# Graph-attention layers on one core: second-layer weights in one VectorE pass, their target factors in values and sum columns, folding on TensorE, and a new step order

## The chip, the cores and the metric

The kernel runs on one core of a Trainium2 chip. Its engines are TensorE (PE in the profile; PEld is its weight load), VectorE (DVE), ScalarE (ACT), GpSimd (POOL) and SyncE (SP), which here only issues transfers. The metric is the device time of one execution in microseconds, lower is better. A comparison counts as a difference from about 0.2% on.

## The reference, cut to what matters

64 graphs of 256 nodes and 512 features go through three attention layers with one shared adjacency `adj` per graph. All is float32.

```python
# layer 0: 8 heads of 64
Q, K, V = x @ W_q + b_q, x @ W_k + b_k, x @ W_v + b_v
scores  = Q K^T / 8 + (x @ w_g[:D])[:, None] + (x @ w_g[D:])[None, :] + log(adj + 1e-9)
x = softmax(scores) V + x
# graph attention, called twice: 8 heads (W1), then 1 head (W2)
h = layer_norm(x) @ W ;  s = h . a_src ;  t = h . a_dst        # per head
e = leaky_relu(s[:, None] + t[None, :], 0.2) + adj
x = softmax(e) h + x
```

Below these are "layer 0", "layer 1" (8 heads) and "layer 2" (one head); the "second layer" of the title is layer 1.

## The kernel before

**A softmax without maxima.** The exponential of leaky_relu(s + t) is max(exp(s + t), exp(0.2 (s + t))). A factor that depends only on the row i (the source, s) drops out of a softmax over j. Dividing by exp(s) leaves, for target j and row i, the larger of e1 = exp(t_j) and e2 R = exp(0.2 t_j) exp(-0.8 s_i), times EA = exp(adj). The rows R = exp(-0.8 s) are made by `target_rows` (L393 to 410): TensorE transposes the column s (called `ends`), ScalarE takes the exponential, the row goes to DRAM and comes back spread over all partitions. The weight tile is made in the transposed position (j on partitions): for each of 8 heads and each half of j ScalarE computes relu(e2 R - e1) (L601), and VectorE adds e1 and multiplies by EA (L605). Layer 2 does it in VectorE alone (L651, L654).

**Sums and values.** `weight_sums` (L338 to 366) lets TensorE multiply weight tiles by columns of ones (`onehot`), 32 columns at a time, so that the sums of eight heads land in one bank; VectorE takes the reciprocal (L355), which goes through DRAM and returns as R, spread over the partitions of each head (L362). `weigh` (L368) multiplies weights by values on TensorE (`num`), and VectorE multiplies by R (L385) and adds bias and residual (L387), giving yT or zT. `tokens` transposes back for the statistics of the layer norm (bn_stats L252, aggregate, variance; a power on POOL, L226), whose result `rstd` scales what leaves the next product.

**Products of 512 x 512 weights** run as seven half-size products instead of eight (`winograd`, L270 to 320). Four sums of blocks of the left factor come from POOL (`left_factors`, L255), those of the weights from `combine` (L94) once. Products 1, 5, 2, 6 and 3 form one step, 7 and 4 one step each. ScalarE copies a partial product out of PSUM ("kept", L467, L490, L560), so that product 6 waits for the copy of product 1; VectorE adds two partial products ("put", L476, L484, L532, L569). Product 4 leaves through ScalarE (L567). For layers 1 and 2 copies and puts also scale by `rstd`.

**Folding.** The layer norm's gain g, bias b and mean are folded into W1 and W2 once, by `fold_norm` (L127 to 216): scaled, the column mean subtracted, two extra columns per head (W times a_src and a_dst) appended, so that s and t come out of the same product as h. Nearly all of that is VectorE work, and it stands in graph 0, ahead of its first use.

**Order.** `graph(b)` is a generator that yields after each step, from "load" to "product 2". TensorE executes steps in an order written by hand, `period`: pairs of an age and a step, so that graphs of six ages, -1 to 4, are in flight in one period. The first and last graphs use the same list with the missing ages left out. Other engines' order is decided by a scheduler, which also assigns buffers[...]. Buffers that matter here: four ET buffers shared by layer 0 and layer 1, eight PSUM banks for everything, four "kept" buffers, and two o2 buffers, shared by the output tile and the final checks. The checks of the range of sums and exponents (L716 to 729) come last and decide how many graphs a plain second pass repeats; here none.

## Time and profile before

| | |
|---|---|
| time, median of 3 | 3669.86 us (3669.45 to 3669.88) |
| span of the profiled run | 3667.4 us |
| chain that ended last, by engine | PE 74%, DVE 17%, ACT 4%, POOL 2%, issue 2%, DMA 1% |
| DMA, mean over the span | 102 GB/s, 32% of 16 engines |
| largest group on ScalarE | L601, 1024 x 597 ns |
| largest group on VectorE | L605, 1024 x 550 ns |
| largest on TensorE | L378, `num`, 4096 records of 382 ns |

How to read it. The records of matmuls overlap[...]: their mean length is longer than the distance from start to start (a product of two 128 x 128 x 264 matmuls has four records, lasts 1.05 us and is followed 0.89 us later by the next one). So busy time is a union, and how long work takes is read from starts. The waits of an engine are listed apart, each with what ended it. A line of a helper (`winograd`, `tokens`) stands for several layers; tiles tell them apart: `wq`, `wk`, `wv` and `w` (layers 1 and 2, 264 and 257 columns wide).

### The profile page before, as it was taken

How to read it: one execution, taken by the hardware profiler on the slowest of the kernel's cores; microseconds unless marked ns; L12 is line 12 of the kernel's file. 1: busy time of each engine (PE TensorE's matmuls, PEld its weight loads, DVE VectorE, ACT ScalarE, POOL GpSimd, SP SyncE). 2: the span in 40 equal slices, each digit the busy share in tenths (PEclk: the TensorE clock that was granted, in tenths of full speed). 3: DMA queues.
4: the chain of work that ended last, by engine and by line, in shares of the span. 5: the costliest groups of instructions: out<-in, count | busy, mean ns of one | idle time of the engine just before them, and what ended most of it. 6: DMA issues, size and time to landing. Idle time of an engine off the chain costs nothing.

```text
span 3667.4 us, 75964 instructions
## 1 busy us (share of the span) xinstructions
PE 3496.0 (95%) x29969; PEld 2907.1 (79%) x29969; DVE 2531.1 (69%) x6015; ACT 1549.5 (42%) x3717; POOL 678.7 (19%) x981
## 2 busy tenths in 40 slices
PE   6989999999999999999999999999999999999995
PEld 5778888888888888888888888888888888888874
DVE  7676676677677667667667766766766766676675
ACT  2434444444444444444444444444444444444441
POOL 1111121121111111111111111211211111111120
PEclk9999999999999999999999999999999999999998
DMA  4323333333323323333333333333333233233331
GB/s 129 94 86 106 101 106 102 105 101 104 107 93 113 106 91 113 103 96 111 100 102 111 97 106 102 103 105 102 103 102 107 94 112 106 90 114 102 97 101 56
DMA packets 202332, 373.90 MB, mean 102 GB/s; under 512 B 21554, under 2 KB 119410, under 8 KB 201972
## 3 DMA queue, kind: packets, MB, share of 16 engines
q1 hardware_dynamic: 198084, 367.67, 31.9%
q8 instruction: 239, 3.92, 0.4%
q10 hardware_dynamic: 3888, 1.32, 0.2%
q14 instruction: 121, 0.99, 0.1%
HBM read 266.61 MB, written 102.31 MB: 101 GB/s over the span
## 4 chain that ended last, share of the span: by engine, by line
PE 74%; DVE 17%; ACT 4%; issue 2%; POOL 2%; DMA 1%; SPq 0%; ACTq 0%; DVEq 0%; POOLq 0%
PE ps_a L286 15%; PE ps_a L293 13%; PE ps_num L378 12%; PE ps_b L286 8%; PE ps_b L293 6%; PE ps_sc L507 5%; PE ps_su L349 3%; PE ps_av L664 3%; DVE ET L517 3%; PE ps_c L286 3%; PE ps_c L293 3%; DVE ET L605 2%; DVE st L252 2%; DVE X L622 2%; ACT ET L514 2%
## 5 line engine op out<-in xcount | busy, mean ns | idle before, releaser
L601 ACT ACTIVATE ET<-R,ne,e 128x256 f32<-128x256 f32 x1024 | 537.5, 597 | 85.9 <-PE ps_num L378 75.8
L605 DVE SCALAR_TENSOR_TENSOR ET<-ET,e,EA 128x256 f32<-128x256 f32 x1024 | 537.2, 550 | 0.2 <-ACT ET L601 0.2
L378 PE MATMUL ps_num<-ET,V 128*64 128x256 f32 x4096 | 470.3, 382 | 0.0
L378 PEld LDWEIGHTS ps_num<-ET,V 128*64 128x64 f32 x4096 | 282.4, 137 | 158.3 <-DVE var L224 18.9
L385 DVE TENSOR_TENSOR ps_num<-ps_num,R 128x512 f32<-128x512 f32 x256 | 177.3, 693 | 314.1 <-PE ps_num L378 187.3
L517 DVE TENSOR_TENSOR ET<-ET,AT 128x1024 f32<-128x1024 f32 x256 | 307.9, 1223 | 92.3 <-ACT ET L514 92.1
L286 PE MATMUL ps_a<-w,S 128*128 128x264 f32 (+1 forms) x1024 | 276.0, 392 | 42.2 <-ACT m L560 42.2
L265 POOL TENSOR_TENSOR S<-yT 128x256 f32<-128x256 f32 x128 | 95.7, 747 | 1059.8 <-DVE yT L387 1049.8
L514 ACT ACTIVATE ET<-ps_sc 128x512 f32<-128x512 f32 x512 | 270.4, 600 | 45.4 <-PE ps_sc L507 45.4
L286 PE MATMUL ps_b<-w,S 128*128 128x264 f32 (+1 forms) x1024 | 268.8, 385 | 16.7 <-DVE w L97 16.7
L286 PE MATMUL ps_a<-w,yT 128*128 128x264 f32 (+1 forms) x1024 | 280.6, 396 | 3.7 <-DVE V L569 3.7
L286 PEld LDWEIGHTS ps_a<-w,S 128*128 128x128 f32 x1024 | 179.6, 190 | 107.7 <-ACT m L560 67.5
L664 PE MATMUL ps_av<-V,ET 128*128 128x258 f32 (+1 forms) x1024 | 248.5, 387 | 11.2 <-DVE ET L654 11.2
L507 PE MATMUL ps_sc<-QT,KT 64*128 64x256 f32 x2048 | 255.7, 389 | 0.0
L560 ACT ACTIVATE m<-ps_a,rstd 128x257 f32<-128x257 f32 (+1 forms) x128 | 61.3, 479 | 457.8 <-POOL rstd L226 240.8
L349 PE MATMUL ps_su<-ET,onehot 128*32 128x128 f32 x8192 | 251.3, 275 | 0.0
L349 PEld LDWEIGHTS ps_su<-ET,onehot 128*32 128x32 f32 x8192 | 216.8, 110 | 29.9 <-issue 21.7
L286 PEld LDWEIGHTS ps_b<-w,S 128*128 128x128 f32 x1024 | 195.1, 191 | 48.4 <-issue 17.4
L664 PEld LDWEIGHTS ps_av<-V,ET 128*128 128x128 f32 x1024 | 198.5, 194 | 42.1 <-DVE ET L654 6.4
L286 PEld LDWEIGHTS ps_a<-w,yT 128*128 128x128 f32 x1024 | 179.3, 190 | 60.5 <-issue 36.2
L507 PEld LDWEIGHTS ps_sc<-QT,KT 64*128 64x128 f32 x2048 | 187.3, 186 | 46.8 <-issue 22.1
L262 POOL TENSOR_TENSOR S<-yT 128x256 f32<-128x256 f32 x128 | 93.7, 732 | 661.4 <-PE ps_a L286 496.2
(161 smaller groups left out, 6440.3 us busy)
## 6 DMA issues: line engine op xcount, KB each, us to landing
xT<-kept SPq DMA_DIRECT2D x128, 512.0 KB
R<-kept SPq DMA_DIRECT2D x256, 256.0 KB
R<-kept SPq DMA_DIRECT2D x128, 512.0 KB
X<-in_x_dram SPq DMA_DIRECT2D x64, 512.0 KB
kept<-xT SPq DMA_DIRECT2D x64, 512.0 KB
kept<-yT SPq DMA_DIRECT2D x64, 512.0 KB
out_dram<-o SPq DMA_DIRECT2D x128, 256.0 KB
A<-in_adj_dram SPq DMA_DIRECT2D x64, 256.0 KB
```

The lines of the kernel that those rows point to most:

```text
L265: nc.gpsimd.tensor_tensor(s3, a11, a21, ALU.subtract)
L286: nc.tensor.matmul(to, A[:, kk, :], B[:, kk, :], start=(first and kk == 0), stop=(kk == 1), skip_group_check=not first,)
L293: nc.tensor.matmul(to[:, m * P : (m + 1) * P], B[:, kk, m * P : (m + 1) * P], A[:, kk, :], start=(first and m == kk == 0), stop=(kk == 1), ...
L349: nc.tensor.matmul(pt[32 * g : 32 * g + 32, :P], onehot[:, i, :], pair[h // 4][:, j, h % 4, o : o + P], start=(i == j == 0), stop=(i == 3 ...
L378: nc.tensor.matmul(at[i * DH : (i + 1) * DH, :], V[:, j, h // 4, h % 4 * DH : (h % 4 + 1) * DH], pair[h // 4][:, j, h % 4, :], start=(j == ...
L385: nc.vector.tensor_tensor(both, both, R[:, m0 : m0 + 2, :], ALU.mult)
L507: nc.tensor.matmul(banks[h % 2][:, o : o + N], KT[lo : lo + DH, (q + h) // 2, j * P : (j + 1) * P], QT[lo : lo + DH, (q + h) // 2, :], sta ...
L514: nc.scalar.activation(ET[:, j, i::2, :], banks[i].rearrange("p (h n) -> p h n", n=N), AF.Exp)
L517: nc.vector.tensor_tensor(ET[:, j, :, :], ET[:, j, :, :], AT[:, j, :].unsqueeze(1).to_broadcast([P, 4, N]), ALU.mult,)
L601: nc.scalar.activation(e, R[q][:, h, :], AF.Relu, scale=e2[:, j, at : at + 1], bias=ne1[:, j, at : at + 1],)
L605: nc.vector.scalar_tensor_tensor(e, e, e1[:, j, at : at + 1], EA[:, j, :], ALU.add, ALU.mult)
L664: nc.tensor.matmul(av[:, :width], ET[:, j, t * P : (t + 1) * P], V2[:, j, n, :width], start=(j == 0), stop=(j == NT - 1),)
```

## The change

It has five parts.

1. **Weights of layer 1 in one pass.** Dividing also by exp(0.2 t_j) leaves max(R, f) EA with f = exp(0.8 t_j): one VectorE operation, no ScalarE one. The missing factor exp(0.2 t_j) belongs to the target, the contracted index: it is multiplied into the values V1 (four VectorE operations a graph) and into the columns that TensorE sums with (`factor_columns`, filled by ScalarE, two sets used in turn). In layer 2 it goes into EA (two ScalarE operations), and the weights are one operation for each half.
2. **Layer 0.** AT = adj + 1e-9 is now a ScalarE operation; exp(c), which was a factor of AT, becomes the bias of the scores' exponential. The range check reads the sums in PSUM rather than their reciprocals.
3. **Folding on TensorE.** `fold_norm` becomes a generator of three steps ("transpose", "columns", "totals"): W is transposed on TensorE to multiply it by a_src and a_dst, sums over rows for bias and mean are matmuls, and VectorE scales and subtracts in one operation per block. The vectors a_src and a_dst come as columns, and POOL spreads them.
4. **Step order.** A new `period`, a written list `start` for the first steps (with the folding in it) and a list `finish` for the last ones.
5. **The range checks** stand after "rows 2" of the last graph rather than after everything.

The diff, cut to its core:

```diff
-    onehot = const.tile([P, 4, 32], F32, name="onehot")
-    nc.gpsimd.memset(onehot, 0.0)
-    for i in range(4):
-        nc.gpsimd.memset(onehot[:, i, 8 * i : 8 * i + 8], 1.0)
+    def sum_columns(name, n):
+        t = const.tile([P, 24 + 32 * n], F32, name=name)
+        nc.gpsimd.memset(t, 0.0)
+        return t, t[:, 24:].rearrange("p (n c) -> p n c", c=32)[:, :, :8]
+    ones, eights = sum_columns("ones", 1)
+    nc.gpsimd.memset(eights, 1.0)
+    factor_columns = [sum_columns(f"factors{i}", NT * H) for i in range(2)]
+    filled = [None, None]
...
+            vectors = const.tile([P, KC, 2, heads], F32, name=f"vectors{name}")
+            nc.gpsimd.memset(vectors, 0.0)
+            for i, a in enumerate((sources, targets)):
+                a = load_columns(f"a{i}{name}", a.rearrange("h d -> (h d)"))
+                for h in range(heads):
+                    lo, hi = (h % 2 * DH, h % 2 * DH + DH) if heads > 1 else (0, P)
+                    chunk = slice(h // 2, h // 2 + 1) if heads > 1 else slice(0, KC)
+                    nc.gpsimd.tensor_copy(vectors[lo:hi, chunk, i, h], a[lo:hi, chunk])
+            yield
+            wT = work.tile([P, KC, D], F32, name="wT", tag="ET", bufs=4)
+            for m in range(KC):
+                pt = ps("fold")
+                for kc in range(KC):
+                    block = w[:, BLOCKS[kc // 2, m // 2], kc % 2, m % 2 * P : m % 2 * P + P]
+                    nc.tensor.transpose(pt[:, kc * P : (kc + 1) * P], block, ident)
+                nc.scalar.copy(wT[:, m, :], pt)
+            yield
+            pt = ps("fold")
+            more = w.shape[-1] - HD
+            products = pt[:, : KC * 2 * heads].rearrange("p (k n) -> p k n", k=KC)
+            for kc in range(KC):
+                for m in range(KC):
+                    nc.tensor.matmul(
+                        products[:, kc, :], wT[:, m, kc * P : (kc + 1) * P],
+                        vectors[:, m].rearrange("p i h -> p (i h)"),
+                        start=(kc == m == 0), stop=(m == KC - 1), skip_group_check=True,
+                    )
+            for (k, n), at in BLOCKS.items():
+                nc.vector.tensor_copy(
+                    w[:, at, :, HD:], products[:, 2 * k : 2 * k + 2, n * more : (n + 1) * more]
+                )
+            yield
+            columns, means = (
+                work.tile([P, KC, P], F32, name=n, tag="o2") for n in ("columns", "means")
+            )
+            nc.scalar.copy(columns, b.unsqueeze(2).to_broadcast([P, KC, P]))
+            nc.scalar.mul(means, g.unsqueeze(2).to_broadcast([P, KC, P]), 1.0 / D)
+            got = {}
+            for what, left in (("row", columns), ("mean", means)):
                 for n in range(2):
-                    part = acc[:, n * HD : (n + 1) * HD]
+                    pt = got[what, n] = ps(what)[:, : HD + more]
                     for kc in range(KC):
-                        block = w[:, BLOCKS[kc // 2, n], kc % 2, :HD]
-                        if kc == 0:
-                            nc.vector.tensor_scalar(part, block, scale(kc), None, ALU.mult)
-                        else:
-                            nc.vector.scalar_tensor_tensor(
-                                part, block, scale(kc), part, ALU.mult, ALU.add
-                            )
-                pt = ps("fold")
-                nc.tensor.matmul(pt, ones, acc, start=True, stop=True)
-                return pt
+                        nc.tensor.matmul(
+                            pt, left[:, kc, :], w[:, BLOCKS[kc // 2, n], kc % 2, :],
+                            start=(kc == 0), stop=(kc == KC - 1),
+                        )
...
+            for kc in range(KC):
+                for n in range(2):
+                    block = w[:, BLOCKS[kc // 2, n], kc % 2, :]
+                    nc.vector.scalar_tensor_tensor(
+                        block, block, g[:, kc : kc + 1], got["mean", n], ALU.mult, ALU.subtract
+                    )
+            combine(w)
...
-        def weight_sums(pair):
+        def weight_sums(pair, columns):
...
+                        t, at = columns(j, h)
                         nc.tensor.matmul(
-                            pt[32 * g : 32 * g + 32, :P], onehot[:, i, :],
+                            pt[32 * g : 32 * g + 32, :P], t[:, at - 8 * i : at - 8 * i + 32],
...
-            note(inverse, 0)
+            note(pt[:, :P], 0)
...
-            for j in range(NT):
-                nc.vector.tensor_scalar(
-                    AT[:, j, :], pt[:, j * N : (j + 1) * N], 1e-9, ec[:, j : j + 1],
-                    ALU.add, ALU.mult,
-                )
+            nc.scalar.activation(AT.rearrange("p j n -> p (j n)"), pt, AF.Identity, bias=eps)
...
-                            ET[:, j, i::2, :], banks[i].rearrange("p (h n) -> p h n", n=N), AF.Exp
+                            ET[:, j, i::2, :], banks[i].rearrange("p (h n) -> p h n", n=N), AF.Exp,
+                            bias=c[:, j : j + 1],
...
-            e1 = small.tile([P, NT, H], F32, name="e1", tag="e1")
-            nc.scalar.activation(e1, ends[:, :, 1, :], AF.Exp)
-            e2 = small.tile([P, NT, H], F32, name="e2", tag="e2")
-            nc.scalar.activation(e2, ends[:, :, 1, :], AF.Exp, scale=0.2)
-            ne1 = small.tile([P, NT, H], F32, name="ne1", tag="ne1")
-            nc.vector.tensor_scalar(ne1, e1, -1.0, None, ALU.mult)
+            f = small.tile([P, NT, H], F32, name="f", tag="f")
+            nc.scalar.activation(f, ends[:, :, 1, :], AF.Exp, scale=0.8)
+            factors, factors8 = factor_columns[b % 2]
+            filled[b % 2] = b
+            for j in range(NT):
+                nc.scalar.activation(
+                    factors8[:, j * H : (j + 1) * H, :],
+                    ends[:, j, 1, :].unsqueeze(2).to_broadcast([P, H, 8]), AF.Exp, scale=0.2,
+                )
+                for n in range(2):
+                    v = V1[:, j, n, :HD].rearrange("p (h d) -> p h d", d=DH)
+                    at = j * H + n * H // 2
+                    nc.vector.tensor_tensor(
+                        v, v, factors8[:, at : at + H // 2, :1].to_broadcast([P, H // 2, DH]), ALU.mult
+                    )
...
-                        e, at = ET[:, j, h, :], 4 * q + h
-                        nc.scalar.activation(
-                            e, R[q][:, h, :], AF.Relu, scale=e2[:, j, at : at + 1],
-                            bias=ne1[:, j, at : at + 1],
-                        )
+                        at = 4 * q + h
                         nc.vector.scalar_tensor_tensor(
-                            e, e, e1[:, j, at : at + 1], EA[:, j, :], ALU.add, ALU.mult
+                            ET[:, j, h, :], R[q][:, h, :], f[:, j, at : at + 1], EA[:, j, :],
+                            ALU.max, ALU.mult,
                         )
...
-            R = weight_sums(pair)
+            assert filled[b % 2] == b
+            R = weight_sums(pair, lambda j, h: (factors, 24 + 32 * (j * H + h)))
...
+            f = small.tile([P, NT], F32, name="f2", tag="f2")
+            nc.scalar.activation(f, ends[:, :, 1, 0], AF.Exp, scale=0.8)
+            factor = small.tile([P, NT], F32, name="factor", tag="factor")
+            nc.scalar.activation(factor, ends[:, :, 1, 0], AF.Exp, scale=0.2)
+            for j in range(NT):
+                nc.scalar.mul(EA[:, j, :], EA[:, j, :], factor[:, j : j + 1])
...
-                nc.vector.tensor_scalar(
-                    ET[:, j, :], R[0][:, 0, :], e2[:, j : j + 1], e1[:, j : j + 1], ALU.mult, ALU.max
+                nc.vector.scalar_tensor_tensor(
+                    ET[:, j, :], R[0][:, 0, :], f[:, j : j + 1], EA[:, j, :], ALU.max, ALU.mult
                 )
-            nc.vector.tensor_tensor(ET, ET, EA, ALU.mult)
...
-            (4, "V2 7"), (2, "rows 1"), (0, "Q"), (3, "weights"), (0, "Q7"), (4, "V2 4"),
-            (3, "weights"), (4, "rows 2"), (4, "weights 2"), (3, "weights"), (0, "Q4"),
-            (2, "weights"), (1, "product 0"), (-1, "load"), (0, "K"), (0, "K7"), (3, "sums 1"),
-            (1, "tokens 1"), (0, "K4"), (0, "scores"), (3, "product 1"), (1, "V1"), (1, "V1 7"),
-            (4, "product 2"), (0, "V"), (1, "V1 4"), (0, "scores"), (0, "V7"), (2, "weights"),
-            (4, "product 2"), (-1, "transpose x"), (3, "tokens 2"), (2, "weights"), (2, "weights"),
-            (0, "V4"), (0, "sums 0"), (3, "V2"), (2, "weights"),
+            (0, "transpose x"), (3, "weights"), (3, "weights"), (3, "weights"), (4, "V2 7"),
+            (0, "Q"), (3, "weights"), (4, "V2 4"), (3, "weights"), (0, "Q7"), (2, "weights"),
+            (4, "rows 2"), (1, "product 0"), (0, "Q4"), (0, "K"), (0, "K7"), (-1, "load"),
+            (3, "sums 1"), (3, "product 1"), (1, "tokens 1"), (4, "weights 2"), (0, "K4"),
+            (0, "scores"), (1, "V1"), (4, "product 2"), (3, "tokens 2"), (1, "V1 7"), (0, "V"),
+            (0, "scores"), (0, "V7"), (3, "V2"), (0, "V4"), (4, "product 2"), (2, "weights"),
+            (1, "V1 4"), (0, "sums 0"), (1, "rows 1"), (2, "weights"),
...
+        start = [
+            (0, "load"), (0, "transpose x"), (0, "Q"), (0, "Q7"), (0, "Q4"), (0, "K"), (0, "K7"),
+            (0, "K4"), (0, "scores"), (0, "V"), (1, "load"), (0, "scores"), ("w1", "transpose"),
+            ("w1", "columns"), (1, "transpose x"), ("w1", "totals"), (0, "V7"), (0, "V4"),
+            (0, "sums 0"), (1, "Q"), (1, "Q7"), (0, "product 0"), (1, "Q4"), (1, "K"), (1, "K7"),
+            (2, "load"), (0, "tokens 1"), (1, "K4"), (1, "scores"), ("w2", "transpose"), (0, "V1"),
+            ("w2", "columns"), (0, "V1 7"), (1, "V"), (1, "scores"), (1, "V7"), (1, "V4"),
...
+        finish = [
+            (-4, "rows 1"), (-5, "weights"), (-2, "transpose x"), (-5, "weights"), (-5, "weights"),
+            (-5, "weights"), (-6, "V2 7"), (-2, "Q"), (-5, "weights"), (-6, "V2 4"),
+            (-5, "weights"), (-2, "Q7"), (-4, "weights"), (-6, "rows 2"), (-3, "product 0"),
+            (-2, "Q4"), (-2, "K"), (-2, "K7"), (-1, "load"), (-5, "sums 1"), (-5, "product 1"),
...
+            (-2, "V2 4"), (-1, "weights"), (-2, "rows 2"), (-1, "sums 1"), (-1, "product 1"),
+            (-2, "weights 2"), (-2, "product 2"), (-1, "tokens 2"), (-1, "V2"), (-2, "product 2"),
+            (-1, "V2 7"), (-1, "V2 4"), (-1, "rows 2"), (-1, "weights 2"), (-1, "product 2"),
+            (-1, "product 2"),
+        ]
+        whole = start + order[len(start) - len(FOLDS) : len(order) - len(finish)]
+        whole += [(B + g, name) for g, name in finish]
...
+                if (g, name) == (B - 1, "rows 2"):
+                    worst = small.tile([P, 1], F32, name="worst", tag="worst")
+                    for v in (top, bottom):
+                        over = work.tile([P, P + 4 * H], F32, name="over", tag="o2")
+                        nc.gpsimd.memset(over, 0.0)
+                        note_odd(over[:, :P], v[:, :P], 1e-25, 1e25)
+                        note_odd(over[:, P:], v[:, P:], -60.0, 60.0)
+                        nc.vector.tensor_reduce(worst, over, AX.X, ALU.max)
+                        nc.vector.tensor_tensor(odd, odd, worst.to_broadcast([P, NT]), ALU.max)
...
```

## The prediction

> **What bounds the kernel now.** I read the engine totals first, then the same totals cut into three stretches, then who TensorE waits for in each stretch, and last the order of events in one period.
>
> ```profile
> PE 3496.0 (95%) x29969; PEld 2907.1 (79%) x29969; DVE 2531.1 (69%) x6015; ACT 1549.5 (42%) x3717; POOL 678.7 (19%) x981
> ```
>
> ```profile
> 0.00:227.84 227.84, 180.50 (x1420) 150.73 (x1420) 159.62 (x377) 77.57 (x187) 35.55 (x60) 0.94 0.34 106
> 227.84:3560.84 3333.00, 3248.85 (x28122) 2707.19 (x28123) 2309.30 (x5456) 1448.78 (x3476) 628.72 (x899) 1.00 0.33 103
> 3560.84:3667.45 106.61, 66.62 (x433) 49.14 (x428) 62.14 (x183) 23.16 (x55) 14.40 (x23) 0.86 0.22 68
> ```
>
> The columns are the stretch, its length, busy PE, PEld, DVE, ACT and POOL, then the clock granted to TensorE. The timeline shows the layer-2 row transpose at 2004.31 and again at 2059.86: a period is 55.55 us, and the middle stretch is 60 of them (3333.0/55.55). In it TensorE waits for two things only:
>
> ```profile
> PE ps_tr L397 <- DVE ends L637: 45.8, 60, 0.8
> PE ps_a L286 <- ACT m L560: 37.7, 59, 0.6
> ```
>
> (total us, times, longest). With 0.6 us of small ones that is 84.1 us, 1.40 a period. So bare TensorE work is (3333.0 - 84.1)/60 = 54.15 us a graph, 3465.6 us for 64. Head and tail take 227.84 + 106.61 = 334.4 us, of which 4 x 54.15 = 216.6 is the same work; 117.8 us is overhead. Its waits, head first, then tail:
>
> ```profile
> PE ps_b L286 <- DVE w L97: 16.7, 2, 11.5
> PE ps_tr L433 <- DMA A<-in_adj_dram: 7.4, 1, 7.4
> PE ps_a L286 <- DVE V L532: 6.7, 4, 3.9
> PE ps_a L293 <- DVE QT L476: 4.9, 4, 2.9
> PE ps_fold L153 <- DVE acc L149: 3.7, 1, 3.7
> ```
>
> ```profile
> PE ps_av L664 <- DVE ET L654: 11.2, 3, 6.1
> PE ps_tr L727 <- DVE worst L724: 8.4, 1, 8.4
> ```
>
> All head waits add to 47.4, all tail waits to 32.2, the time after the last matmul to 7.6, the old folding matmuls to 5.9 (4.6 + 1.3). The remaining 24.7 is slow clock and small losses. VectorE needs 2309.3/60 = 38.5 us a period and ScalarE 24.1: neither bounds.
>
> [...] 97.5% busy in the middle stretch does not say what the matmuls could do, so I price from waits and from start-to-start times. [...] after the 11.46 us wait at 92.84 a product took 2.10 us, in the steady state 1.05. [...] ScalarE's first arithmetic waits 7.95 us behind its own weight-vector loads. [...] the rows at L201 took 434.
>
> **The change part by part.**
>
> First-layer weights. Gone on ScalarE: 16 x 597 ns = 9.55 us a graph.
>
> ```profile
> L601 ACT ACTIVATE ET<-R,ne,e 128x256 f32<-128x256 f32 x1024 | 537.5, 597 | 85.9 <-PE ps_num L378 75.8
> L605 DVE SCALAR_TENSOR_TENSOR ET<-ET,e,EA 128x256 f32<-128x256 f32 x1024 | 537.2, 550 | 0.2 <-ACT ET L601 0.2
> ```
>
> The VectorE pass keeps its shape, 16 x 550 ns. ScalarE also gains AT (597, as the EA row), two scalings of EA (2 x 597) and two 64-wide exponentials (between 199 and 363 each), and loses e1 and ec (216 + 204): net about -7.7, to 16.5 us. VectorE loses AT (2 x 475), ne (174) and layer-2 weights (2 x 597 + 676), and gains layer-2 weights (2 x 550) and four scalings of V1 (4 x 434): net -0.15. The note of the sums moves from SBUF to PSUM at the same shape. None of this is on the path: TensorE waits for neither in 54 of 55 us. The sums on TensorE use other columns, same 32-column weights: 0. So this part makes room, and by itself gives about nothing.
>
> Step order. TensorE's work per graph is the same; what counts is which waits the order leaves. (a) The row transpose waits 0.77 us after the last layer-2 product, for one ScalarE and one VectorE step. Now product 7 of Q (0.89 us) stands between them: hidden, 0.12 to spare. (b) Layer-2 product 6 waits 0.64 for the statistics of tokens 2. Before, V4, sums 0 and three products (0.97 + 1.88 + 2.6 = 5.5 us) lie between; now V1 7, five V products, scores, V7 and three products: 0.9 + 4.35 + 1.93 + 0.9 + 2.6 = 10.7. Hidden. New tight places: (c) V1 follows tokens 1 with only K4, scores and three products between, 0.98 + 1.93 + 2.7 = 5.6, against 5.5 + 0.64 = 6.1 that the other chain needed, less two residual additions (2 x 0.6) that this one does not have, 4.9. (d) Transposing x stands right ahead of V2 7 and Q. Product 5 needs AT, two copies (about 0.55 each start to start) and two POOL operations (0.73): 0.44 + 0.6 + 1.1 + about 0.95 = 3.1 us, and TensorE arrives after 1.31 + 0.97 + 0.89 = 3.2. (e) Product 1 follows sums 1 at once; its multiplication waits in VectorE's queue for R:
>
> ```profile
> 2017.45 0.94 DVE L355 RECIPROCAL inverse<-ps_su 128x128 f32<-128x128 f32 x1
> ...
> 2025.13 0.70 DVE L385 TENSOR_TENSOR ps_num<-ps_num,R 128x512 f32<-128x512 f32 x1 [2.01 <-DMA R<-kept]
> ```
>
> That is 7.7 us from sums to R. Behind it queue the additions that make zT, the second masking of the scores and the V1 puts. TensorE meanwhile has product 1, tokens 1, K4 and scores, 3.6 + 1.0 + 1.0 + 1.9 = 7.5; the multiplication then follows the first masking, which itself ends some 8.9 us after the sums. zT is done near 11.7; TensorE gets to tokens 2 after V1 and a product 2, at 7.5 + 4.5 + 1.8 = 13.8. Hidden, 2 us spare. I keep 0.1 us a period for these: 6 us.
>
> Folding. Per layer 20 transposes (8 take 0.87: 2.2 us), 16 matmuls onto 2 or 16 columns (not in the trace; [...] at most the 0.22 of a 128-column one; I take 0.22: 3.5) and 16 of 264 columns (0.445: 7.1): 12.8, twice 25.6 us instead of 5.9. Of the head's waits 16.7, 3.7, 1.4 (for bw) and 5.3 of those on V go, since VectorE then has eight 0.49 us operations and the four of combine (0.7) per layer instead of some seventy; I add 3.5 for copies of the transposed weights and for V4 behind the folding. Against it, four more vector loads sit ahead of ScalarE's first copies, and POOL spreads those vectors before it makes Q's factors. Such a load took 7.2 us (issued 2.35, landed 9.55). Issue then ends near 14.5 instead of 9.6, the last lands near 22, and Q's second product starts near 23 instead of 15.6; 2.9 us of that was waited for the wv loads anyway. I add 4.5 (bounds 0 and 8). Head waits: 47.4 - 27.1 + 3.5 + 4.5 = 28.3.
>
> Tail. The range checks (8.4 us behind the last output) move ahead of it: -7.8. Layer-2 weights are one pass shorter, 0.7 x 3: -2. The finish list fills some waits: -3. Tail: 39.8 - 12.8 = 27. Slow clock: without the three long waits 24.7 becomes 18.
>
> Sum: 3465.6 + 6 + 28.3 + 25.6 + 27 + 18 = **3570 us**.
>
> **The rivals.** *A wait takes the place of the removed one* at (c), (d) or a PSUM bank: 0.7 us a period, 3570 + 42 = 3612. For it: (c) and (d) have little to spare. Against: ScalarE is a third emptier. *More is hidden*: folding fills time in which TensorE waits anyway (-20) and the finish list does more (-10): 3540. *R holds VectorE's queue*: if its round trip grows by 4 us (adjacency, x and the wide R loads are near it), the masking, V1 and tokens 2 all slip, some 2.5 us a period: 3570 + 150 = 3720, slower. For it: R already ends a wait of 2.01 us in the kernel before. Against: 2 us to spare.
>
> **How the numbers follow.** Forecast 0.60, moved wait 0.20, more hidden 0.12, R 0.07, no change 0.01. The range reaches from the "more hidden" case to the moved wait: 3540 to 3612. Faster 0.92, same 0.01, slower 0.07.
>
> **What would show it.** Right: a period of 54.2 to 54.3 us with neither of the two waits; ScalarE near 17 us and VectorE near 38 a period; TensorE's first Q product after 15 us; folding matmuls of some 25 us; no long wait on w; checks ahead of the last output. Wrong: a new wait on m, S or a put in every period, or VectorE idle on R for over 3 us a period.

## The result, and the profile after

The changed kernel takes **3585.82 us** (median of 4 runs, 3585.27 to 3586.28) against 3669.65 us beside it (4 runs): a ratio of 0.9773, with a 95% interval of 0.9756 to 0.979. The prediction was 3570 us. The sum came out within 16 us, in part by luck: two errors in it cancel, and the head came out for another reason than the one given. One argument did not hold: the part that was said to bring about nothing by itself is worth 72 to 122 us with the rest of the change in.

The engine totals of the page after: TensorE's busy time is what it was (3496.0 before), in a span 83 us shorter.

```profile
PE 3496.4 (98%) x30121; PEld 2949.6 (82%) x30121; DVE 2498.9 (70%) x5899; ACT 1200.0 (33%) x2897; POOL 689.0 (19%) x999
```

The same totals by stretch, cut where the layer-1 row transpose starts (at 270.01 and again at 3411.93). Columns: stretch, length, busy PE, PEld, DVE, ACT, POOL, clock granted to TensorE, DMA share, GB/s.

```profile
0.00:270.01 270.01, 243.17 (x1961) 208.20 (x1962) 147.83 (x331) 86.14 (x200) 46.21 (x89) 0.95 0.32 96
270.01:3411.93 3141.92, 3119.78 (x27148) 2638.51 (x27145) 2244.64 (x5279) 1080.44 (x2610) 616.13 (x870) 1.00 0.35 106
3411.93:3584.20 172.27, 133.45 (x1021) 102.85 (x1017) 106.45 (x291) 33.42 (x87) 26.65 (x40) 0.91 0.28 82
```

The middle is 58 periods, 3141.92/58 = **54.17 us** each instead of 55.55. VectorE works 2244.64/58 = 38.7 us a period, ScalarE 18.6. What TensorE waits for (total us, times, longest), the middle first:

```profile
PE ps_b L291 <- POOL S L260: 22.1, 58, 0.4
```

Both old waits are gone from the middle and one small new one has come, in every period: product 5 of Q waits for GpSimd's factor S. The largest of the head that the change brought, then those of the tail that the text below uses:

```profile
PE ps_b L291 <- POOL S L260: 6.4, 2, 5.9
```

```profile
PE ps_tr L243 <- DVE yT L387: 9.7, 3, 4.5
PE ps_av L663 <- DVE ET L651: 6.8, 3, 5.8
PE ps_tr L796 <- DVE worst L793: 0.8, 1, 0.8
```

All waits of the head add to 26.6 us, all of the tail to 31.1. The wait for the range checks has fallen from 8.4 to 0.8 us.

### The profile page after: what moved, and what is told of

Same layout as the page of the kernel before. It is cut to its first block, busy times and chain, and to the rows that moved or that the text cites. A ratio compares the mean times of both kernels' runs of the same rounds, so it can differ in the third digit from the quotient of the medians.

```text
span 3584.2 us, 75284 instructions
## 1 busy us (share of the span) xinstructions
PE 3496.4 (98%) x30121; PEld 2949.6 (82%) x30121; DVE 2498.9 (70%) x5899; ACT 1200.0 (33%) x2897; POOL 689.0 (19%) x999
## 3 DMA queue, kind: packets, MB, share of 16 engines
q1 hardware_dynamic: 198084, 367.67, 33.9%
q8 instruction: 241, 3.95, 0.5%
## 5 line engine op out<-in xcount | busy, mean ns | idle before, releaser
L603 DVE SCALAR_TENSOR_TENSOR ET<-R,f,EA 128x256 f32<-128x256 f32 x1024 | 515.0, 543 | 9.7 <-DMA R<-kept 6.4
L508 ACT ACTIVATE ET<-ps_sc,c 128x512 f32<-128x512 f32 x512 | 309.7, 687 | 143.9 <-PE ps_sc L501 143.9
L250 DVE BATCH_NORM_STATS2 st<-ps_tr 128x6 f32<-128x512 f32 x256 | 165.7, 688 | 172.5 <-PE ps_tr L243 172.5
L284 PE MATMUL ps_a<-w,S 128*128 128x264 f32 (+1 forms) x1024 | 268.4, 385 | 3.5 <-ACT m L553 3.5
L385 DVE TENSOR_TENSOR ps_num<-ps_num,R 128x512 f32<-128x512 f32 x256 | 171.6, 693 | 121.8 <-PE ps_num L378 82.9
L260 POOL TENSOR_TENSOR S<-yT 128x256 f32<-128x256 f32 x128 | 103.5, 809 | 626.6 <-PE ps_a L284 530.0
L263 POOL TENSOR_TENSOR S<-yT 128x256 f32<-128x256 f32 x128 | 93.3, 729 | 626.3 <-DVE yT L387 530.3
L224 POOL TENSOR_TENSOR rstd<-var,mhalf 128x2 f32<-128x2 f32 x128 | 89.7, 701 | 544.1 <-DVE var L222 544.1
L291 PE MATMUL ps_b<-S,wq 128*128 128x128 f32 x1024 | 142.4, 282 | 28.9 <-POOL S L260 28.9
L476 ACT COPY KT<-ps_a 128x256 f32<-128x256 f32 x64 | 23.8, 372 | 433.2 <-DVE st L250 415.3
```

The lines of the kernel that those rows point to most:

```text
L250: nc.vector.bn_stats(st, pt)
L260: nc.gpsimd.tensor_tensor(s1, a21, a22, ALU.add)
L263: nc.gpsimd.tensor_tensor(s3, a11, a21, ALU.subtract)
L284: nc.tensor.matmul(to, A[:, kk, :], B[:, kk, :], start=(first and kk == 0), stop=(kk == 1), skip_group_check=not first,)
L291: nc.tensor.matmul(to[:, m * P : (m + 1) * P], B[:, kk, m * P : (m + 1) * P], A[:, kk, :], start=(first and m == kk == 0), stop=(kk == 1), ...
L385: nc.vector.tensor_tensor(both, both, R[:, m0 : m0 + 2, :], ALU.mult)
```

## The experiments

Every run is a median beside runs of the kernel before, whose medians were 3669.7 to 3671.9 us. These medians differ by 2 us, and the kernel after was not run again beside the later ones, so a difference of 5 to 10 us between two rows is known to about 2 us. "Period" below is the median distance between layer-1 row transposes in the steady part of each trace.

| kernel | time, us | ratio to before (95% interval) | period, us |
|---|---|---|---|
| before | 3669.65 | | 55.55 |
| after | 3585.82 | 0.9773 (0.9756 to 0.979) | 54.17 |
| old order, new weights | 3735.7 | 1.0173 (1.0156 to 1.019) | 56.72 |
| new order, old weights | 3708.33 | 1.0113 (1.009 to 1.0137) | 56.0 |
| old order, old weights | 3807.53 | 1.0376 (1.0358 to 1.0393) | 58.7 in about half, 57.14 in the others |
| new order, layer-1 weights old | 3614.23 | 0.9847 (0.9832 to 0.9862) | 54.51 |
| old order, scratch moved | 3699.39 | 1.0079 (1.0064 to 1.0095) | 56.10 |
| no lists | 3596.19 | 0.9795 (0.9778 to 0.9811) | 54.17 |
| checks last | 3593.81 | 0.9788 (0.9772 to 0.9804) | 54.17 |
| s1 early | 3560.18 | 0.97 (0.9684 to 0.9716) | 53.75 |
| x first | 3553.56 | 0.9678 (0.9662 to 0.9695) | 53.62 |
| vectors late | 3580.52 | 0.9755 (0.9738 to 0.9771) | 54.18 |
| wide fold | 3579.95 | 0.9753 (0.9737 to 0.9769) | 54.17 |
| three edits together | 3541.59 | 0.9651 (0.9638 to 0.9664) | 53.62 |

### Order or weights?

**Old order, new weights.** The after kernel with the following (in outline, the lists are long):

```diff
-        whole = start + order[len(start) - len(FOLDS) : len(order) - len(finish)]
-        whole += [(B + g, name) for g, name in finish]
+        period = [ (4, "V2 7"), (2, "rows 1"), (0, "Q"), ... ]     # the list of the kernel before
+        whole = order, with the three "w1" steps after (0, "sums 0") and the three "w2" steps after (0, "sums 1")
```

> The kernel after with everything but the order: the step order of the kernel before, no first-steps and last-steps lists, the three folding steps of each layer run in one piece where the folding stood before (after sums 0 and sums 1 of the first graph). My theory: the order removes the waits, the one-pass weights do not. Then the period stays near the old one, 55.2 to 55.6 us, with the row transpose waiting about 0.8 us and layer-2 product 6 about 0.6 us in every period, and the time is 3640 to 3675 us. Rival: the emptied ScalarE is what shortens the period. Then at least one of the two waits is gone here too, the period is 54.8 us or less, and the time is under 3625 us.

Measured: 3735.7 us, period 56.72. Both old waits are there, so the order is what removes them. But the kernel is 64 us *slower than before*, which neither theory had. The wait of layer-2 product 6 is now 1.81 us in every period instead of 0.64. The timeline of this kernel from the last transposes of tokens 2 (TensorE starts the next product at 1798.24) to product 6 (start, duration, engine, line, output and inputs, and in brackets the idle time of the engine and what ended it):

```profile
1799.41 0.68 DVE L424 CUSTOM_DVE_ANT_0 AT<-X,wc 128x512 f32<-128x512 f32 x1
...
1800.19 0.69 ACT L433 ACTIVATE AT<-ps_tr,eps 128x512 f32<-128x512 f32 x1 [5.11 <-DVE odd L334]
...
1800.78 1.06 ACT L445 COPY xT<-ps_tr 128x512 f32<-128x512 f32 x2
...
1803.83 0.72 POOL L262 TENSOR_TENSOR S<-xT,S 128x256 f32<-128x256 f32 x1
1804.51 0.70 POOL L224 TENSOR_TENSOR rstd<-var,mhalf 128x2 f32<-128x2 f32 x1
...
1805.24 0.48 ACT L553 ACTIVATE m<-ps_a,rstd 128x257 f32<-128x257 f32 x1 [3.12 <-POOL rstd L224]
...
1805.77 1.14 PE L284 MATMUL ps_a<-w,S 128*128 128x257 f32 x4 [1.81 <-ACT m L553]
```

Read it downwards. The change lets VectorE write the product of x and wc into AT, because only its sum is wanted and the old scratch buffer (`junk`) is gone. AT itself is now written by ScalarE, and so ScalarE must wait until VectorE has made both sums. (The releaser printed is the neighbour VectorE instruction that finished last.) The copies of x stand behind AT in ScalarE's queue, four operations on S behind those on GpSimd, and the scale rstd behind S. A chain across three queues that the kernel before did not have ends in product 6.

**The scratch moved.** To test that chain, the old order with one more edit:

```diff
+            scratch = work.tile([P, NT, N], F32, name="scratch", tag="ET2", bufs=1)
...
-                    out=AT.rearrange("p j n -> p (j n)"), in0=X[:, t, :], in1=wc, scale=1.0, scalar=0.0,
+                    out=scratch.rearrange("p j n -> p (j n)"), in0=X[:, t, :], in1=wc, scale=1.0, scalar=0.0,
```

> The kernel with the old step order and the new arithmetic (3736 us), but the product of x with wc, of which only the sum is used, is written into the buffer of the layer-2 weights and not into AT. Theory A: with the product in AT, ScalarE cannot write AT until VectorE has made both sums, the copies of x stand behind AT on ScalarE, GpSimd's four operations on S behind these, and the scale of tokens 2 behind those; that is what raised the wait of layer-2 product 6 from 0.64 to 1.81 us. AT then starts about 2.4 us earlier, the scale is set by VectorE's statistics alone, about 0.7 us earlier, the wait is near 1.1 us, and the time 3690 to 3700 us. Theory B: VectorE's own queue makes the statistics late (the sums now stand ahead of them), and freeing ScalarE changes nothing: 3730 to 3740 us.

Measured: 3699.39 us, 36 less, with product 6 waiting 1.02 us. Theory A holds in size. The scale now waits for VectorE's variance and no longer behind S:

```profile
1731.50 0.70 POOL L224 TENSOR_TENSOR rstd<-var,mhalf 128x2 f32<-128x2 f32 x1 [0.88 <-DVE var L222]
```

Product 6 still waits longer than the 0.64 us of the kernel before. A reading for this rest, which was not tried: VectorE now makes both sums of x (1725.50 and 1727.03) ahead of the statistics, where in the kernel before it made them behind (from 2051.22 on), and the variance ends 2.7 us after the start of product 1 instead of 2.0.

In the new order the same shared buffer holds nothing up, because x's sums are made about 6 us ahead of AT (VectorE ends them at 1997.97, ScalarE starts AT at 2004.35).

**New order, old weights.** The after kernel, with the weights of layers 1 and 2 made as before:

```diff
-                        nc.vector.scalar_tensor_tensor(
-                            ET[:, j, h, :], R[q][:, h, :], f[:, j, at : at + 1], EA[:, j, :], ALU.max, ALU.mult)
+                        nc.scalar.activation(e, R[q][:, h, :], AF.Relu, scale=e2[:, j, at : at + 1], bias=ne1[:, j, at : at + 1])
+                        nc.vector.scalar_tensor_tensor(e, e, e1[:, j, at : at + 1], EA[:, j, :], ALU.add, ALU.mult)
...
-                nc.vector.scalar_tensor_tensor(ET[:, j, :], R[0][:, 0, :], f[:, j : j + 1], EA[:, j, :], ALU.max, ALU.mult)
+                nc.vector.tensor_scalar(ET[:, j, :], R[0][:, 0, :], e2[:, j : j + 1], e1[:, j : j + 1], ALU.mult, ALU.max)
+            nc.vector.tensor_tensor(ET, ET, EA, ALU.mult)
```

> The kernel after with the attention weights of both layers made as before (layer 1: a ScalarE Relu, then a VectorE pass; layer 2: two VectorE passes; no factor in the values, sums by columns of ones), in the new step order with its lists. My theory: the order does not need the free ScalarE. ScalarE rises from about 18.6 to 25 or 26 us a period, still under half of it, the period is 54.2 to 54.5 us, and the time 3585 to 3605 us. Rival: with ScalarE full the new tight places wait (the copies of x ahead of Q's factors, the copies ahead of layer-2 product 6), 0.7 us or more a period, and the time is 3630 us or more.

Measured: 3708.33 us, far on the rival's side, though not at the places that the rival named. The new order needs the new weights. The trace shows where:

```profile
1863.86 1.21 DVE L642 TENSOR_TENSOR ET<-ET,EA 128x512 f32<-128x512 f32 x1
...
1865.10 0.60 ACT L433 ACTIVATE EA<-ps_tr 128x512 f32<-128x512 f32 x1 [2.32 <-DVE ET L642]
...
1866.02 1.92 PE L289 MATMUL ps_a<-S,wk 128*128 128x128 f32 x8 [1.89 <-ACT u L482]
```

Four buffers hold EA. A new graph's EA must wait until the layer-2 weights of the graph four ahead have been made, and here these take 1.13 + 1.21 us on VectorE instead of one pass over each half. While ScalarE waits 2.32 us for the buffer, the copy u behind it in the queue waits too, and K's product 7 with it: 76.7 us in all, over 59 waits. The one shown is among the longest: of the 56 waits of 1 us and more between 280 and 3400 us, half last 1.23 us or less. The product after it took 1.92 us, where it takes 1.16 after most of these waits; 4 of the 56 were followed by such a slow one.

**Only layer 1 old.** The same with layer 2 left in one pass.

> The kernel after with only the layer-1 attention weights made as before (ScalarE Relu, then VectorE; no factor in the values, sums by columns of ones); layer 2 keeps its one pass. With both layers' old weights the time was 3708 us, and TensorE waited 77 us for the copy u of K's fourth product, which stood behind the exponential EA on ScalarE; EA waited for the layer-2 weights on VectorE to free its buffer. Theory A: layer 2's two passes, 1.2 us longer on VectorE, hold that buffer; with layer 2 in one pass the wait is gone and the time is 3590 to 3620 us. Theory B: the 16 Relus of layer 1 in ScalarE's and VectorE's queues shift everything behind them, and the wait for u stays: 3680 us or more.

Measured: 3614.23 us, as theory A had it. So of the 122 us, the old form of layer 2 costs 94 us on top of an old layer 1, most of it by way of EA's buffer: TensorE waits for u 4.1 us in all here instead of 76.7. The old form of layer 1 alone costs 28 us. ScalarE then works 933.87 instead of 689.20 us in a stretch of 2000, and TensorE waits for a copy m ahead of product 6, 20.8 us in all over 63 waits; how the 28 us come about was not taken apart. Layer 2 alone in its old form was not run.

**Both old.** The last corner of the square.

> The old step order and the attention weights of both layers as before, with everything else of the kernel after (AT by ScalarE, its buffer taking the product of x with wc, folding on TensorE, checks ahead of the end). It closes the square of weights and order: new weights and new order 3586 us, new weights and old order 3736, old weights and new order 3708. Theory A, as the prediction had it: the form of the weights is worth nothing in the old order, and what makes the old order slower is AT's place; then this takes 3720 to 3750 us, with layer-2 product 6 waiting about 1.8 us a period. Theory B: the one-pass weights, whose work on VectorE stands at other places than the old passes, are what the old order cannot bear; then this falls back to 3650 to 3685 us and the wait to about 0.7 us.

Measured: 3807.53 us, above both ranges. The wait of product 6 has grown again, and the mean clock granted to TensorE is 0.981 (0.995 in the old order with the new weights). In 28 of 52 periods of the middle the product is slow after the wait (2.08 us at 1258.94, for instance; period 58.7 to 58.9 us); where it takes 1.14 us, as here, the period is 57.14:

```profile
1771.22 3.05 ACT L591 ACTIVATE ET<-R,ne,e 128x256 f32<-128x256 f32 x6
...
1774.65 0.59 ACT L443 COPY xT<-ps_tr 128x512 f32<-128x512 f32 x1 [0.38 <-PE ps_a L282]
...
1776.65 0.69 ACT L431 ACTIVATE AT<-ps_tr,eps 128x512 f32<-128x512 f32 x1 [1.41 <-DVE c L422]
...
1777.23 0.58 ACT L443 COPY xT<-ps_tr 128x512 f32<-128x512 f32 x1
...
1781.54 1.14 PE L282 MATMUL ps_a<-w,S 128*128 128x257 f32 x4 [2.23 <-ACT m L551]
```

Six Relus now stand ahead of the first copy of x, and AT ahead of the second. The square, all four with AT on ScalarE, folding on TensorE and the checks ahead of the end:

| | old order | new order | the order brings |
|---|---|---|---|
| old weights | 3807.5 | 3708.3 | 99 |
| new weights | 3735.7 | 3585.8 | 150 |
| the weights bring | 72 | 122 | |

The old order of this square also does without the two lists, which with the folding's place are worth 10 us (below). The corner of both old is 137 us above the kernel before. So the rest of the change is a loss in the old order, each main part on top of it still leaves the kernel slower than before, and only both together win, by 51 us more than their sum.

### The new wait for S

Product 1 to product 5 of Q should take 0.89 us from start to start. In the kernel after it takes 1.43:

```profile
2004.35 0.69 ACT L433 ACTIVATE AT<-ps_tr,eps 128x512 f32<-128x512 f32 x1
...
2004.94 1.06 ACT L445 COPY xT<-ps_tr 128x512 f32<-128x512 f32 x2
...
2005.60 0.82 POOL L263 TENSOR_TENSOR S<-xT 128x256 f32<-128x256 f32 x1 [4.64 <-ACT xT L445]
...
2005.90 1.05 PE L291 MATMUL ps_a<-xT,wq 128*128 128x128 f32 x8
...
2006.38 0.90 POOL L260 TENSOR_TENSOR S<-xT 128x256 f32<-128x256 f32 x1
...
2007.33 1.16 PE L291 MATMUL ps_b<-S,wq 128*128 128x128 f32 x8 [0.38 <-POOL S L260]
```

GpSimd makes s3 (L263) first, since it needs only the first copy of x. s1 (L260), for which product 5 waits, comes second; and both copies stand behind AT.

**s1 early.**

```diff
-            nc.gpsimd.tensor_tensor(s3, a11, a21, ALU.subtract)
+            nc.gpsimd.tensor_tensor(s3, a22, s2, ALU.subtract)
```

> The kernel after with one of Q's and K's and all later left factors made from others: s3 = a22 - s2 in place of a11 - a21 (the same matrix), so that GpSimd can no longer make s3 ahead of s1, which product 5 waits for. My theory: GpSimd's 0.8 us on s3 stands between the second copy of x and s1, so s1 comes 0.4 to 0.7 us earlier and the wait in every period is gone. From the start-to-start times the wait delays product 5 by 0.54 us (1.43 from product 1 to product 5 instead of 0.89), not by the 0.38 recorded as idle, so the gain is 58 to 60 x 0.54, about 32 us: near 3554 us. Rival 1: only the recorded idle time is lost, 60 x 0.38 = 23 us: 3563 us. Rival 2: product 7, which now gets s3 last, or the next step waits in its place, and the gain is under 5 us.

Measured: 3560.18 us (3557.27 to 3564.09), a gain of 26 us, period 53.75. By the time alone Rival 1 (3563 us) is nearer than the theory (3554 us). The starts decide: the wait is gone from the record, but product 5 still starts 1.01 us after product 1. So 0.42 us a period are gained, more than the 0.38 recorded as idle, and 0.12 stay, in a delay that shows no idle time. The expected 32 us was too much, because GpSimd's s1 ends at 1831.13 here and product 5 starts at 1831.18.

**x first.** The block that transposes and copies x stands ahead of the one for the adjacency (in outline):

```diff
+            xT = data.tile([P, KC, N], F32, name="xT", tag="xT")
+            for k0 in range(0, KC, 2): ...
             pt = ps("tr")
             for j in range(NT): ...
             nc.scalar.activation(AT.rearrange("p j n -> p (j n)"), pt, AF.Identity, bias=eps)
...
-            xT = data.tile([P, KC, N], F32, name="xT", tag="xT")
-            for k0 in range(0, KC, 2): ...
```

> The kernel after with the transposes and copies of x ahead of those of the adjacency in the step that transposes x. The copies that GpSimd needs then start on ScalarE about 0.44 us (four transposes) and one 0.6 us copy earlier. My theory: the wait for S is gone in every period, and the head gains a little, since x lands ahead of the adjacency: 3550 to 3556 us. Rival 1: ScalarE or the bank of the adjacency is then late for the next user, and 0.3 us or more a period come back: 3570 us. Rival 2: no change in the middle because GpSimd, not ScalarE, is the limit: 3585 us.

Measured: 3553.56 us, 32 less, as expected: 58 x 0.55. Only the head gained nothing: its second product waits 7.25 us for S instead of 5.90. In the middle product 5 now starts 0.88 us after product 1:

```profile
1827.05 1.05 PE L291 MATMUL ps_a<-xT,wq 128*128 128x128 f32 x8
...
1827.93 1.06 PE L291 MATMUL ps_b<-S,wq 128*128 128x128 f32 x8
```

### Head, folding and tail

**Vectors late.** The four attention vectors are loaded on SyncE's queue behind the weights, and spread after K7 of the first graph (cut: `load_columns` takes the queue as an argument):

```diff
-                a = load_columns(f"a{i}{name}", a.rearrange("h d -> (h d)"))
+                a = load_columns(f"a{i}{name}", a.rearrange("h d -> (h d)"), nc.sync)
...
+                if (g, name) == (0, "K7"):
+                    for key in ("w1", "w2"): next(graphs[key])
```

> The kernel after with the four attention-vector loads on SyncE's queue behind the weights and their spreading on GpSimd after the first graph's K7. My theory: in the head the spreading holds GpSimd for 7.6 us (18 copies) and the loads hold ScalarE's queue for about 2 us, so the second product starts near 16 us instead of 22.6 and the time falls by 6 to 9 us: 3577 to 3580 us. Rival: TensorE then waits for the next thing, the V weights or the scores' copies, and gets back under 2 us: 3584 us or more.

Measured: 3580.52 us, 5.3 less. The row of the kernel after that held S, and the second product of Q with it moved out of the way (22.61 in the kernel after):

```profile
13.56 7.64 POOL L152 COPY vectors<-a 64x1 f32<-64x1 f32 x18 [10.52 <-DMA a<-in_L_gnn_a_src_dram]
```

```profile
15.78 2.07 PE L291 MATMUL ps_b<-S,wq 128*128 128x128 f32 x8 [0.59 <-POOL S L260]
```

That is 6.8 us earlier, of which 1.5 are lost later. The gain falls just short of the range of 6 to 9 us.

**Wide fold.** The 16 narrow matmuls of each folding on 128 columns each, the added ones zero (cut to the matmul):

```diff
-                        nc.tensor.matmul(products[:, kc, :], wT[:, m, kc * P : (kc + 1) * P],
-                            vectors[:, m].rearrange("p i h -> p (i h)"), ...)
+                        nc.tensor.matmul(products[:, kc, :], wT[:, m, kc * P : (kc + 1) * P], wide[:, m], ...)
```

> The kernel after with the 16 narrow matmuls of each folding run on 128 columns, the added ones zero, instead of 16 and 2. My theory: [...] with 128 columns each takes 0.22 us, 3.5 us a layer instead of 5.4 and 4.1, and the clock stays up: 6 to 9 us less, 3577 to 3580 us. Rival: [...] the clock falls because of the waits for the copies around it; then 128 columns bring nothing or cost 1 us: 3585 to 3587 us.

Measured: 3579.95 us, 5.9 less, and the reason shows. Busy times and clock around layer 2's folding (matmuls of 2 columns from 96.96 to 101.27), the kernel after, then with 128 columns (92.82 to 96.39); the clock is the column of 1.00, 0.64, 0.50:

```profile
96.90:99.00 2.10, 2.10 (x21) 2.07 (x20) 0.49 (x1) 0.00 (x0) 0.00 (x0) 1.00 0.00 0
99.00:101.00 2.00, 2.00 (x14) 2.00 (x14) 0.00 (x0) 0.00 (x0) 0.00 (x0) 0.64 0.03 8
101.00:104.00 3.00, 3.00 (x8) 2.44 (x9) 0.85 (x5) 0.00 (x0) 0.00 (x0) 0.50 0.00 0
```

```profile
92.80:95.00 2.20, 2.20 (x21) 2.18 (x20) 0.49 (x1) 0.00 (x0) 0.00 (x0) 1.00 0.00 0
95.00:97.00 2.00, 2.00 (x17) 1.94 (x17) 0.36 (x4) 0.00 (x0) 0.00 (x0) 1.00 0.03 8
97.00:100.00 3.00, 3.00 (x16) 2.62 (x15) 0.49 (x1) 0.74 (x2) 0.00 (x0) 1.00 0.00 0
```

PE is "busy" throughout in both, and no wait stands ahead of the 2-column run. Doing 64 times the columns, the wide run takes 3.57 us where the narrow one takes 4.31, because the narrow one loses the clock midway and leaves it low for the products after it. As long as it had the full clock, a narrow record followed the last after 0.11 us, just as a wide one does. In layer 1 the run falls from 6.00 to 4.47 us; there the first matmuls wait for the copies of W in both kernels.

**No lists.** The new period from the first graph to the last, each layer's folding in one piece after sums 0 of the first and of the second graph.

> The kernel after without the first-steps and last-steps lists: the new period runs from the first graph to the last, with the three folding steps of each layer in one piece after sums 0 of the first and of the second graph. My theory: the middle stays at 54.17 us a period, and only head and tail lose: the last graphs leave their waits unfilled (I put 3 us on the finish list), and the folding stands in one piece with its copies waited for, 3 to 8 us: 3590 to 3600 us. Rival: the lists do most of what the head and tail gained, and without them 20 us or more are lost, 3606 us or more.

Measured: 3596.19 us, 10 more: both lists with the folding's place are worth 10 us. They were not tried apart, but the trace parts them. The fifth layer-1 row transpose stands at 332.15 us instead of 324.18, so 8.0 us go in the head; from the 63rd to the end it is 120.0 us instead of 118.1, so the list of the last steps is worth 1.9. The largest wait of the tail is what it was with the list:

```profile
PE ps_tr L243 <- DVE yT L387: 9.7, 3, 4.1
```

**Checks last.** The block of range checks back behind the loop.

> The kernel after with the range checks back behind everything. My theory: they come back as a VectorE chain behind the last output that TensorE's last transpose waits for, 7.8 us: 3592 to 3595 us. Rival: the end of the kernel is set by the last output's own transfer and the checks run beside it, 3586 to 3588 us.

Measured: 3593.81 us, 8.0 more, and `worst` is waited for as long as in the kernel before:

```profile
PE ps_tr L794 <- DVE worst L791: 8.4, 1, 8.4
```

**Three edits together**: x first, vectors late, wide fold.

> The kernel after with three edits at once: x's transposes and copies ahead of the adjacency's (alone 3553.6 us), the attention vectors' loads and spreading later (alone -5.3 us), the narrow folding matmuls on 128 columns (alone -5.9 us). My theory: the three lie in different places and add up, 3553.6 - 5.3 - 5.9 = 3542 us, or 1 to 2 us less, since with x first the second product of the head waited 7.2 us for S and not 5.9. Rival: the head is set by the arrival of the weights, and moving one wait uncovers another there: 3548 us or more.

Measured: 3541.59 us (5 runs, 3540.78 to 3544.16), which beats both kernels: 44 us below the kernel after, 3.5% below the one before. The edits add up. 3100 us of its middle:

```profile
268.00:3368.00 3100.00, 3100.00 (x27068) 2626.87 (x27065) 2250.29 (x5263) 1077.02 (x2594) 612.51 (x866) 1.00 0.34 107
```

TensorE does not wait at all there, and a period is 53.62 us. What is left above 64 x 53.62 = 3432 us is head and tail.

## Why the prediction was right, and where it was not

The terms of its sum, against the span of the profiled run (3584.2 us):

| term | predicted | measured | from |
|---|---|---|---|
| bare TensorE work, 64 graphs | 3465.6 | 3431.7 | 64 x 53.62, a period without waits |
| waits left in the periods | 6 | 33.0 | 60 x (54.17 - 53.62) |
| head waits | 28.3 | 26.6 | sum of the head |
| folding matmuls | 25.6 | 29.5 | start to start: transposes 4.6, narrow 10.3, totals 14.5 |
| tail | 27 | 38.6 | waits 31.1, after the last matmul 7.5 |
| slow clock and small losses | 18, the author's estimate | 24.8 | what remains |

**Bare work and waits: two errors that cancel.** The step "(3333.0 - 84.1)/60 = 54.15" took recorded idle time for the whole cost of a wait. It is not. In the kernel before, product 6 of layer 2 starts 1.67 us after product 2, with 0.64 us of idle recorded:

```profile
2047.99 1.03 PE L286 MATMUL ps_c<-w,yT 128*128 128x257 f32 x4
...
2049.66 1.14 PE L286 MATMUL ps_a<-w,S 128*128 128x257 f32 x4 [0.64 <-ACT m L560]
```

The row transpose starts 1.80 us after the product ahead of it (2002.51 to 2004.31), with 0.77 recorded. Without a wait either step takes 0.87 us, so the two delays are 0.80 and 0.93 us and not 0.64 and 0.77. In the kernel after, product 5 is 0.54 us late with 0.38 us of idle recorded, and in the s1 kernel 0.12 us late with none. In these four places only the starts tell the delay. So bare work was 0.53 us a period too high. Against that, tight place (d) was named, with 3.1 us needed and 3.2 to be had, and kept at a tenth of a microsecond; it cost 0.55. The need was 3.6 us (product 5 at 2007.33, the transposes from 2003.72), and TensorE was there after 3.1: the copies ended 2.3 us after the transposes began (said 2.1), and GpSimd, whose two operations took 0.82 and 0.90 us here and not 0.73, was still busy with s3 for 0.4 us then and gave s1 1.3 us after the second copy (said 0.95). This is the moved-wait rival in kind (S in every period), at less than its 0.7 us, and "a new wait on m, S or a put in every period" is what the prediction itself named as a sign of being wrong. That the sum came out all the same is luck: bare work was 33.9 us too high and the waits 27.0 us too low.

**The step order** did what (a) and (b) said: neither old wait is in any period. (c) and (e) cost TensorE nothing in the middle. R did hold VectorE's queue at the multiplication (L385), 18 times, 38.9 us in all and 3.0 at most; in the kernel before it was 46 times and 95.7 us. The R rival did not come.

**"By itself gives about nothing"** did not hold. The argument was that TensorE waits for neither ScalarE nor VectorE for 54 of 55 us. That is a share, and what counts is the place. With the rest of the change in, the one-pass weights are worth 72 us in the old order and 122 in the new. Two things were missed: AT and the scaling of EA were counted as ScalarE time alone, not as work ahead of the copies of x in ScalarE's queue; and layer 2's pass, priced at a fraction of a microsecond on VectorE, sets when EA's buffer comes free. The pass on its own in the kernel before, without AT's move, was not tried, so the claim is refuted only with the rest of the change in place.

**Folding.** A narrow matmul was priced at its upper bound of 0.22 us, and that is what it takes at full clock (two records, 0.11 us each from start to start). The narrow runs still cost 3.3 us more (10.3 instead of 7.0): 0.9 is layer 1's wait for the copies of W, which the wide run has too, and the rest the clock. What a run of them does to the clock had no term.

**The head** came out by another way than the one given. The second product started at 22.6 us where 23 was said. But ScalarE's issue ended at 11.9 us, not near 14.5, and no copy on GpSimd after the first waited for a load, where the last was said to land near 22. What held GpSimd to 21.2 us were its 18 copies, 7.64 us, which had no price. The first product started at 14.6, not after 15.

**The tail** was missed by 11.6 us. The checks gave their 8 us (8.0 by the run that puts them back), and layer 2's waits fell from 11.2 to 6.8. But the last graphs now wait 9.7 us for yT where it was 2.3 (L245 before, L243 after). The finish list was said to fill waits (3 us). Without the lists the yT waits are the same 9.7 us, and in the old order with the new weights they are 3.3 us in the whole run: they come with the new period.

**ScalarE and VectorE**: 18.6 and 38.7 us a period, said 17 and 38. The Relus were taken off as 16 x 597 ns = 9.55 us, but their records overlap: their busy time is 537.5 us for 64 graphs, 8.4 each. The exponential of the scores with its bias takes 687 ns, 600 without, 0.7 us a period; the four scalings of V1 take 540 ns on the mean (418 the median) and not 434. None of this is on the path.

## What to carry to other kernels

When an engine is far from full, moving work onto or off it can still be worth several per cent, since here what stood behind a waiting instruction waited too (EA's 2.32 us on ScalarE held the copy u behind it, and TensorE for 1.89): ask for each moved instruction what it waits for, what stands behind it, and which buffer it frees. Test the parts of a change in a square, each with and without the other, because here each main part alone, with the small ones, was slower than the old kernel. Measure bare work by start-to-start times between instructions that did not wait, and let the work that a waiting engine needs first be made first: one block moved ahead of another was worth 32 us.

## What the runs showed of the hardware

- In layer 2's folding TensorE's clock fell to half during a run of matmuls with few columns, although the profile shows the engine busy: 32 records onto 2 columns, 4.31 us, clock 0.50 from about 2.6 us on for 6.8 us, through the next three products (2.11, 1.91 and 1.77 us). With 128 columns the clock stayed at 1.00 and the three took 1.06, 1.03 and 1.03 us.
- After some waits near 2 us the next product was slow. Between 280 and 3400 us, of seven waits of 1.88 to 1.90 us (new order, old weights) four were followed by a slow product (one took 1.92 us instead of 1.16); of 53 waits of 2.23 or 2.24 us (both old) 29 were, and of 53 waits of 1.80 to 1.84 us (old order, new weights) none. The mean granted clock of these three runs was 0.993, 0.981 and 0.995. What decides among equal waits is not shown.
- GpSimd's 18 small copies (64x1 and 128x4) took 7.64 us in the busy start of the kernel and 3.95 us when they came later, in the run with the vectors late. Later that is 0.22 us a copy on the mean; in the start eight took 0.56 to 0.69 us, and during each of them VectorE was at one of its two-input operations of 0.69 us on wq, wk or wv.
- A wait can delay a matmul without any idle time in the record: 0.12 us for product 5 of Q in the s1 kernel.
